# One of seven self-feature products by matmuls of 64 and 128 output columns in place of 32

## Chip, cores and metric

The kernel runs on one core of a Trainium2 chip. The metric is the device time of one execution in microseconds, the median of several runs. All data are 32-bit floats, apart from an integer adjacency.

## What is computed

The reference is a graph-attention layer over 16 batches, each with N = 512 nodes and F = 512 features. Cut to what matters:

```
q_exp     = where(x.sum(-1) == 0, 0, q)                  # (B, N, Q)
self_feat = concat([x, q_exp], -1) @ W_self.T + b_self   # (B, N, F)
output    = self_feat
for d in range(2):                                       # the two directions of the adjacency
    kv  = self_feat[:, :20]
    aff = (self_feat @ Wq[d].T + bq[d]) . (kv @ Wk[d].T + bk[d]) per head / sqrt(32)
    aff = where(mask_d, aff, -9e15) + label_bias_d       # 16 heads, 20 keys
    w   = softmax(aff, -1)
    output += (w @ kv) @ Wout[d] per head + bout[d]
out = x + relu(output)
```

The change touches the largest dense product in it, the part of self_feat that multiplies x with the first 512 columns of W_self.

## The kernel before

A setup of about 90 us loads the weights and works out for all 16 batches what depends only on the 20 key nodes: the keys folded into the query weights, the values folded into the output weights, and the self features of batch 0. The setup uses matmuls of several widths: 128 output columns (`key_rows`, line 581; `row_flags`, line 186; part of `values`, line 644), 64 (the other part of `values`, line 644) and 32 (`self_feat`, line 202). "Output columns" are the columns of the stationary operand, so they are the partitions of PSUM that the matmul writes.

Then a loop runs over batch `b` and over four tiles `nt` of 128 nodes each. The order of the instructions on every engine is the order of the program text (`manual_schedule`). For a pair (b, nt) TensorE does, in this order:

- nt = 0: `product(b, 4)`, `scores` (line 353), `product(b, 3)`
- nt = 1: `scores`
- nt = 2: `attend(b - 1)` (line 426, the weighted values of the batch before), `scores`, `product(b + 1, 1)`, `product(b + 1, 2)`
- nt = 3: `product(b + 1, 6)`, `scores`, `product(b + 1, 7)`, `product(b + 1, 5)`

`scores` issues 64 matmuls of 32 output columns and 152 moving columns. VectorE, ScalarE and GpSimd turn a tile of scores into weights by a softmax, and `turn` transposes them for `attend`. `attend` issues 24 matmuls on 32 of the 128 rows, 16 of them 32 columns wide and 8 of them 64 wide.

Self features of batch b + 1 are made in the loop during batch b, by seven products in the manner of Strassen and Winograd: W and the 492 nodes beyond the first 20 are cut in two by two blocks, of 256 x 256 weights and 256 x 246 inputs, and seven block products take the place of eight. `product` (line 279) makes one block product: `i` counts the two 128-row halves of the output, `k` the two halves of the contraction, and `a` four strips of 32 output columns, which write the four groups of 32 PSUM partitions. So a product is 16 matmuls, in the order (i, k) = (0,0), (0,1), (1,0), (1,1) with four strips each. Product 2 has a PSUM bank of its own, `ps_d`; `joined` (line 296) on VectorE reads it in nt = 3. The other products add up in `ps_a` and `ps_c`.

[...] The strips of one (i, k) appear pass by pass: four records of the first pass almost at once, then four of the second. In what follows a *pass* is such a group of strips that run beside each other. A batch has 392 matmuls, or 1568 records, and about 10 semaphore instructions on TensorE, 1578 in all.

The product loop before, whose strips are `R` = 32 columns wide (`HL` = 4 of them, `P` = 128):

```
for i in range(2):
    for k in range(2):
        for a in range(HL):
            at = i * P + a * R
...
            nc.tensor.matmul(to, lhs, x[:, k], start=start, stop=stop, skip_group_check=n != 2)
```

Of the kernel before, what the change touches and what calls it, by code (L numbers as in the profile page):

```python
# [13 lines left out]
P = 128  # L14
# [4 lines left out]
def gat_kernel(  # L19
# [21 lines left out]
    B, F, N = xT.shape  # L41
# [3 lines left out]
    HL = P // DH  # L45
# [6 lines left out]
    R = P // HL  # L52
    HN = (N - NG) // 2
# [12 lines left out]
    def bank(name, at=None):  # L66

        tag = {} if at is None else {"bufs": 1}
        return acc["pool"].tile([P, 512], F32, tag="acc" if at is None else f"acc{at}", name=name, **tag)
# [3 lines left out]
    ws_v = const.tile([P, C, F], F32, name="ws_v")  # L73
    ws_s = const.tile([P, 4, 2, F // 2], F32, name="ws_s")
# [17 lines left out]
    sums, parts, us, done = {}, {}, {}, {}  # L92
# [139 lines left out]
    def x_block(b, j, l):  # L232
        return xs[b][:, 2 * j : 2 * j + 2, half(l)]
# [12 lines left out]
    def product(b, n):  # L246

        w, x = {
            1: ((0, 0), lambda: x_block(b, 0, 0)),
            2: ((0, 1), lambda: x_block(b, 1, 0)),  # L250
            3: (3, lambda: x_block(b, 1, 1)),
            4: ((1, 1), lambda: sums[b, 4]),
            5: (0, lambda: sums[b, 1]),
            6: (1, lambda: sums[b, 2]),
            7: (2, lambda: sums[b, 3]),
        }[n]
        x = x()
        if n == 1:
            parts[b, "a"] = [bank(f"ps_a{b}_{i}", i) for i in range(2)]
        if n == 2:  # L260
            parts[b, "d"] = bank(f"ps_d{b}", 2)
        if n == 5:
            parts[b, "c"] = bank(f"ps_c{b}", 3)
        for i in range(2):
            for k in range(2):
                for a in range(HL):
                    at = i * P + a * R
                    if isinstance(w, tuple):
                        lhs = ws_v[:, 2 * w[1] + k, bass.ds(w[0] * F // 2 + at, R)]
                    else:  # L270
                        lhs = ws_s[:, w, k, bass.ds(at, R)]
                    if n in (2, 3, 5):
                        to = parts[b, "d" if n == 2 else "c"][bass.ts(a, R), bass.ts(i, HN)]
                        start = k == 0 if n == 2 else (n, i, k) == (5, 0, 0)
                        stop = k == 1 if n == 2 else (n, i, k) == (3, 1, 1)
                    else:
                        to = parts[b, "a"][i][bass.ts(a, R), :HN]
                        start, stop = (n, k) == (1, 0), (n, k) == (4, 1)
                    nc.tensor.matmul(to, lhs, x[:, k], start=start, stop=stop, skip_group_check=n != 2)  # L279
# [489 lines left out]
    with tc.manual_schedule():  # L769
# [11 lines left out]
        for b in range(B):  # L781
# [7 lines left out]
            for nt in range(NT):  # L789
# [22 lines left out]
                if nt == 0:  # L812
                    if b == 0:
                        for g in range(2):
                            scores(b, nt, g, ps[g])
                        mask_sum(b, 1)
                    else:
                        mask_mul(b, 1)
                        product(b, 4)
                        for g in range(2):  # L820
                            scores(b, nt, g, ps[g], range(2))
                        normal(*prev)
                        partial(b, 4, 1, 0, block(b, 1, 0))
                        if more:
                            load_x(b + 1, range(2), done["exp"])
                            load_x(b + 1, range(2, C), done["partial"])
                        for g in range(2):
                            scores(b, nt, g, ps[g], range(2, C))
                        if more:
                            row_mask(b + 1)  # L830
                        mask_count(b, 1)
                        joined(b, 3, "c", 1, 1)
                        product(b, 3)
                        mask_sum(b, 1)
                        if more:
                            load_adj(b + 1, 0, done["masks"])
# [46 lines left out]
                if nt == 2:  # L883
                    if more:
                        mask_mul(b + 1, 0)
                    else:
                        full_add(b, NT - 1)
                    if b > 0:
                        banks = [bank(f"ps_o{b - 1}_{q}", q) for q in range(4)]
                        attend(b - 1, banks)  # L890
                        o = work.tile([P, C, N], F32, tag="o", name=f"o{b - 1}")
                        finish(b - 1, o, banks)
                        if b + 2 < B:
                            load_xn(b + 2, 0, done["add"])
                            load_xn(b + 2, 1, done["relu"])
                    normal(*prev)
                    for g in range(2):
                        scores(b, nt, g, ps[g])
                    if more:
                        product(b + 1, 1)  # L900
                        product(b + 1, 2)
                    s = weigh(b, nt, pair, (lambda: partial(b + 1, 1, 0, 0)) if more else None)
                    expo(s)
                    turn(*prev)
                    if b > 0 and more:
                        load_keys(b + 1, range(2), done["exp"])
                    if more:
                        full_add(b, NT - 1)
                    if b > 0:
                        for c in (0, 1):  # L910
                            residual(b - 1, c, o)
# [53 lines left out]
        b = B - 1  # L965
# [22 lines left out]
        for q in (2, 3):  # L988
            w = (NT - 1) * P
# [56 lines left out]
```

## Time and profile before

| | |
|---|---|
| median of 3 runs | 591.74 us (591.52 to 592.68) |
| the profiled execution, whole | 593.27 us |
| its span, first to last instruction | 591.5 us |
| TensorE matmuls busy | 578.7 us, 98% of the span |
| TensorE weight loads busy | 439.7 us, 74% |
| VectorE busy | 492.3 us, 83% |
| ScalarE busy | 395.6 us, 67% |
| GpSimd busy | 384.2 us, 65% |
| mean granted TensorE clock | 0.995 |

The page of the profile gives busy time by engine, the chain of work that ended last, and the costliest groups of instructions. A row of the timeline reads: start and duration in us, engine, line, operation, output<-inputs, rows*columns of the stationary operand, shape of the moving operand, and the number of records merged into the row. A matmul row lasts from its first record's start to its last record's modelled end; since matmuls overlap, the time that a stretch takes on TensorE is the distance from its start to the start of the next stretch. "issue" as a releaser stands for a wait that the profile can't put down to any semaphore.

### The profile page before, as it was taken

The page shows a single profiled execution, that of the slowest core. Times are in us where ns is not written, and L with a number is a line of the kernel's source. Part 1 is how long each engine was busy: PE and PEld are TensorE (multiplying, and loading weights), DVE is VectorE, ACT ScalarE, POOL GpSimd, SP SyncE. Part 2 cuts the span into 40 slices and gives each one's busy share as a digit, 9 for nine tenths or more (in the row PEclk, how much of TensorE's full clock was granted, in tenths as well). Part 3 has the DMA queues.
Part 4 walks back from the last instruction along what each step waited for, and adds up shares of the span by engine and source line. Part 5 has one row for each costly group of instructions (what it writes and reads, how often), then busy time and mean ns, then how long its engine had stood idle before and what let it go on. Part 6 is the DMA issues. An engine that isn't in the chain of part 4 may idle for free.

```text
span 591.5 us, 30038 instructions
## 1 busy us (share of the span) xinstructions
PE 578.7 (98%) x13180; PEld 439.7 (74%) x13180; DVE 492.3 (83%) x785; ACT 395.6 (67%) x1162; POOL 384.2 (65%) x351
## 2 busy tenths in 40 slices
PE   8999999999999999999999999999999999999994
PEld 6654547888978687787878787788787878787882
DVE  0495565889898888999999999888989898989896
ACT  1234644587877677768686868677787877777661
POOL 2315663638677675758686777675858677776774
PEclk9999999999999999999999999999999999999997
DMA  8998999857848485767676766757585748582503
GB/s 294 385 406 299 332 376 329 257 126 199 223 154 229 155 236 148 206 168 209 184 208 163 223 173 202 171 181 208 164 217 170 216 149 232 158 238 85 167 13 142
DMA packets 98129, 124.10 MB, mean 210 GB/s; under 512 B 19952, under 2 KB 70160, under 8 KB 95952
## 3 DMA queue, kind: packets, MB, share of 16 engines
q1 hardware_dynamic: 96752, 120.31, 67.1%
q8 instruction: 103, 1.69, 1.2%
q0 software_dynamic: 672, 1.36, 1.0%
q10 hardware_dynamic: 576, 0.53, 0.3%
q14 instruction: 26, 0.21, 0.1%
HBM read 82.30 MB, written 40.24 MB: 207 GB/s over the span
## 4 chain that ended last, share of the span: by engine, by line
PE 94%; DVE 3%; DMA 1%; issue 1%; ACT 0%; POOL 0%; SPq 0%; DVEq 0%; POOLq 0%; ACTq 0%
PE ps_s L353 44%; PE ps_a L279 17%; PE ps_c L279 8%; PE ps_o L426 6%; PE ps_d L279 4%; PE ps_v L644 3%; PE ps_k L581 3%; PE ps_sf L202 2%; DMA ws_q<-in_wsT 1%; PE ps_kv L532 1%; DVE o L435 0%; PE ps_nz L186 0%; DVE wt L415 0%; DVE ps_s L371 0%; DVE sm L406 0%
## 5 line engine op out<-in xcount | busy, mean ns | idle before, releaser
L353 PEld LDWEIGHTS ps_s<-g,sf 128*32 128x32 f32 x8192 | 264.0, 110 | 19.8 <-issue 12.2
L353 PE MATMUL ps_s<-g,sf 128*32 128x152 f32 x8192 | 277.3, 293 | 0.5 <-ACT st L684 0.5
L334 ACT COPY both<-add 32x80 f32<-32x80 f32 x512 | 130.9, 256 | 54.8 <-DVE add L325 49.0
L408 POOL TENSOR_TENSOR s<-s,sm 128x640 f32<-128x640 f32 x63 | 80.3, 1275 | 98.0 <-DVE sm L407 98.0
L341 POOL TENSOR_TENSOR full<-cq,both 128x640 f32<-128x640 f32 x64 | 100.1, 1565 | 30.3 <-issue 24.3
L314 ACT ACTIVATE prod<-adj,wb_sb 128x80 f32<-128x80 int32 x330 | 112.5, 432 | 0.0
L380 ACT ACTIVATE s<-s 128x640 f32<-128x640 f32 x63 | 46.5, 738 | 69.4 <-DVE s L375 69.0
L444 POOL TENSOR_TENSOR o<-o,x 128x512 f32<-128x512 f32 x60 | 75.9, 1285 | 0.0
L367 DVE TENSOR_TENSOR full<-ps_s,full 128x608 f32<-128x608 f32 x63 | 49.1, 779 | 32.1 <-PE ps_s L353 26.6
L406 DVE TENSOR_REDUCE sm<-s 128x32 f32<-128x640 f32 x63 | 50.9, 808 | 8.8 <-ACT s L380 8.6
L279 PE MATMUL ps_a<-t,ws_s 128*32 128x246 f32 x960 | 55.5, 370 | 0.0
L371 DVE TENSOR_REDUCE ps_s<-full 128x32 f32<-128x640 f32 x63 | 52.2, 828 | 2.2
L415 DVE STREAM_TRANSPOSE wt<-s 128x640 f32<-128x640 f32 x63 | 52.8, 839 | 0.1
L375 DVE TENSOR_TENSOR s<-full,ps_s 128x640 f32<-128x640 f32 x63 | 51.6, 818 | 1.1
L426 PE MATMUL ps_o<-wt,vd 32*32 32x512 f32 (+5 forms) x816 | 40.8, 581 | 3.7 <-DVE wt L400 2.0
L279 PEld LDWEIGHTS ps_a<-t,ws_s 128*32 128x32 f32 x960 | 32.2, 110 | 15.5
L325 DVE TENSOR_REDUCE add<-prod 128x80 f32<-128x960 f32 x32 | 36.8, 1150 | 6.3 <-ACT prod L314 4.4
L244 POOL TENSOR_TENSOR t<-x 128x492 f32<-128x492 f32 x30 | 34.4, 1148 | 10.1 <-DVE full L367 5.2
L439 ACT ACTIVATE o<-o,bo 128x512 f32<-128x512 f32 x60 | 38.2, 708 | 0.6 <-POOL biased L881 0.6
L435 DVE TENSOR_TENSOR o<-ps_o,sf 128x512 f32<-128x512 f32 x60 | 36.8, 672 | 1.0 <-PE ps_o L426 1.0
L286 DVE SCALAR_TENSOR_TENSOR u<-nz,qw,ps_a 128x246 f32<-128x246 f32 x90 | 36.6, 449 | 0.0
L244 POOL TENSOR_TENSOR t<-x,t 128x492 f32<-128x492 f32 x30 | 34.4, 1147 | 1.2
(238 smaller groups left out, 722.7 us busy)
## 6 DMA issues: line engine op xcount, KB each, us to landing
g_d<-st SPq DMA_DIRECT2D x16, 1064.0 KB, 5.9
g<-g_d SPq DMA_DIRECT2D x28, 608.0 KB, 5.2
out_T<-o SPq DMA_DIRECT2D x60, 256.0 KB, 4.7
xn<-in_xn SPq DMA_DIRECT2D x28, 512.0 KB, 3.6
x<-in_xT SPq DMA_DIRECT2D x28, 512.0 KB, 4.3
adj<-in_adj SPq DMA_DIRECT2D x32, 440.0 KB, 5.0
nz<-nz_d SPq DMA_DIRECT2D x14, 256.0 KB, 4.0
wk<-in_wkT SPq DMA_DIRECT2D x2, 1024.0 KB, 8.0
```

The lines of the kernel that those rows point to most:

```text
L244: nc.gpsimd.tensor_sub(t, one, two)
L279: nc.tensor.matmul(to, lhs, x[:, k], start=start, stop=stop, skip_group_check=n != 2)
L314: nc.scalar.activation(p[:, :, l], a[:, :, l], AF.Identity, scale=wb_sb[:, l : l + 1])
L334: nc.scalar.copy(adds[b, h][bass.ts(a, R), :, g], add[r].rearrange("p (t m) -> p t m", t=2))
L341: nc.gpsimd.tensor_add(f, cqs[b].unsqueeze(1).to_broadcast(shape), adds[b, nt // 2][:, nt % 2].unsqueeze(2).to_broadcast(shape),)
L353: nc.tensor.matmul(bank[bass.ts(a, R), bass.ts(j, WD // HL)], sfs[b][:, k, bass.ds(nt * P + (2 * g + j) * R, R)], keys[:, k, a], start=(k ...
L371: nc.vector.tensor_reduce(mx, f, AX.X, ALU.max)
L375: nc.vector.tensor_sub(s, f, mx.unsqueeze(3).to_broadcast(full))
L408: done["normal"] = nc.gpsimd.tensor_mul(s, s, sm.unsqueeze(3).to_broadcast(full))
L415: nc.vector.transpose(wts[b][:, nt], s.rearrange("p a h m -> p (a h m)"))
L426: nc.tensor.matmul(banks[a][bass.ds(at // 2 * DH, n * DH)].rearrange("p (t n) -> p t n", n=32), vd[r, bass.ds(at * DH, n * DH)], wt[r, :, ...
L444: nc.gpsimd.tensor_add(o[:, c], o[:, c], xs[b][:, c])
```

## The change

In `product`, the strips of product 2 become wider: 64 columns where i == k, 128 where i != k. So product 2 has 6 matmuls in place of 16: two of 64 columns, then one of 128, one of 128, and two of 64. The weights that are read, the PSUM cells that are written and the order of i and k stay as they were. The six other products keep strips of 32. A batch has 382 matmuls, 1528 records, and 1538 TensorE instructions with the semaphore instructions. Fifteen product 2 are made in the loop, one for each batch but the first. Nothing changes in the instructions of the other engines or in the setup.

```
-                for a in range(HL):
-                    at = i * P + a * R
+                wide = (2 * R if i == k else P) if n == 2 else R
+                for a in range(P // wide):
+                    at = i * P + a * wide
                     if isinstance(w, tuple):
-                        lhs = ws_v[:, 2 * w[1] + k, bass.ds(w[0] * F // 2 + at, R)]
+                        lhs = ws_v[:, 2 * w[1] + k, bass.ds(w[0] * F // 2 + at, wide)]
                     else:
-                        lhs = ws_s[:, w, k, bass.ds(at, R)]
+                        lhs = ws_s[:, w, k, bass.ds(at, wide)]
                     if n in (2, 3, 5):
-                        to = parts[b, "d" if n == 2 else "c"][bass.ts(a, R), bass.ts(i, HN)]
+                        to = parts[b, "d" if n == 2 else "c"][bass.ts(a, wide), bass.ts(i, HN)]
```

## The prediction

> **What bounds the kernel now.** I read the page first: busy time, the chain that ended last, and the DMA queues.
>
> ```profile
> span 591.5 us, 30038 instructions
> PE 578.7 (98%) x13180; PEld 439.7 (74%) x13180; DVE 492.3 (83%) x785; ACT 395.6 (67%) x1162; POOL 384.2 (65%) x351
> ...
> q8 instruction: 103, 1.69, 1.2%
> ...
> PE 94%; DVE 3%; DMA 1%; issue 1%; ACT 0%; POOL 0%; SPq 0%; DVEq 0%; POOLq 0%; ACTq 0%
> ```
>
> TensorE carries 94% of the chain. A busy TensorE isn't a bound by itself, so the second view is what TensorE waited for inside the loop (from 108 to 560 us):
>
> ```profile
> PE ps_o L426 <- issue: 1.4, 3, 0.5
> PE ps_d L279 <- issue: 0.8, 1, 0.8
> ```
>
> It waits for no other engine and no transfer, only four times for "issue". So a microsecond added to or taken from TensorE's stream in the loop reaches the end, and no slack elsewhere hides it. All 15 changed products lie there. Third, the timeline of TensorE around product 2 in one batch (start, duration, and so on):
>
> ```profile
> 139.85 1.88 PE L279 MATMUL ps_a<-x,ws_v 128*32 128x246 f32 x32
> 141.51 1.88 PE L279 MATMUL ps_d<-x,ws_v 128*32 128x246 f32 x32
> 143.17 1.89 PE L279 MATMUL ps_a<-t,ws_s 128*32 128x246 f32 x32
> ```
>
> From start to start a product takes 1.66 us for 32 records, which is 8 passes of four strips, 0.2075 us a pass. Weight loads lie beneath them.
>
> **Part 1: the streaming doesn't change.** The setup has passes of all three widths. Two visits of one width with different numbers of passes give the price of a pass, and what a visit costs beyond its passes:
>
> ```profile
> 27.04 0.29 PE L669 MATMUL ps_g(0, 0, 0, 0, 2)0_268<-khD,wq_sb 32*128 32x152 f32 x2
> 27.28 2.42 PE L581 MATMUL ps_k<-kvT,wk 128*128 128x320 f32 x8
> ...
> 41.62 1.98 PE L644 MATMUL ps_v<-wo_sb,kvT 128*128 128x512 f32 x4
> 43.53 0.40 PE L669 MATMUL ps_g(0, 3, 1, 1, 2)0_409<-khD,wq_sb 32*128 32x152 f32 x2
> 51.47 1.08 PE L644 MATMUL ps_v<-wo_sb,kvT 128*64 128x512 f32 x4
> 52.48 0.52 PE L669 MATMUL ps_g(1, 2, 0, 0, 2)0_500<-khD,wq_sb 32*128 32x304 f32 x2
> 56.36 1.12 PE L186 MATMUL ps_nz<-rx,ones 128*128 128x512 f32 x2
> 57.41 0.61 PE L202 MATMUL ps_sf<-x,ws_v 128*32 128x236 f32 x8
> 57.95 0.78 PE L669 MATMUL ps_g(1, 3, 1, 0, 2)0_552<-khD,wq_sb 32*128 32x304 f32 x4
> 71.62 1.80 PE L202 MATMUL ps_sf<-x,ws_v 128*32 128x236 f32 x32
> 73.35 0.40 PE L669 MATMUL ps_g(2, 3, 0, 1, 2)0_727<-khD,wq_sb 32*128 32x152 f32 x2
> 82.84 1.13 PE L186 MATMUL ps_nz<-rx,ones 128*128 128x512 f32 x2
> 83.90 1.94 PE L644 MATMUL ps_v<-wo_sb,kvT 128*64 128x512 f32 x8
> 85.77 0.40 PE L669 MATMUL ps_g(3, 2, 0, 1, 2)0_841<-khD,wq_sb 32*128 32x152 f32 x2
> ```
>
> - 128 wide, 512 moving columns: 4 passes take 43.53 - 41.62 = 1.91, 2 passes 57.41 - 56.36 = 1.05. A pass is 0.43, and 0.20 is left over.
> - 64 wide, two strips beside each other: 4 passes take 85.77 - 83.90 = 1.87, 2 passes 52.48 - 51.47 = 1.01. A pass is 0.43 again, 0.15 is left over.
> - 32 wide, 236 columns: 8 passes take 1.73, 2 passes 0.54. A pass is 0.199, 0.14 is left over.
>
> 0.43 for 512 columns and 0.199 for 236 lie on one line (0.83 ns a column), which gives 0.2075 for the 246 of a product: a pass costs the same at each width. Product 2 has two passes for each of its four (i, k) before and after, 8 in all. So 480 matmul records become 180, and the streaming time stays 1.66 us. The records taken away cost nothing where they were; they ran beside others.
>
> **Part 2: four switches of width are added, 0.64 us a batch.** The left-over is paid once per visit. One part is a wait as a width is left: the last pass of 152 columns begins at 27.04, streams for 0.13 (by the line above) and the next width's first record comes at 27.28, so about 0.1 is wait. The rest, 0.04 to 0.1, must be a longer first pass. It isn't the change of rows that costs: 82.84 to 83.90 (left for 64 wide) and 56.36 to 57.41 (left for 32 wide) keep 128 rows on both sides and still cost 0.2 beyond two passes. Before, product 2 was part of one long visit to width 32. Now there are a visit to 64, one to 128, another to 64, and a second visit to 32 after it: 0.15 + 0.20 + 0.15 + 0.14 = 0.64 us. Product 2 so takes 2.30 us; times 15, **+9.6 us**. The steps 64 to 128 and 64 to 32 with 128 rows don't occur in the trace. Bounds: at the cheapest visit for all four, 4 x 0.14 x 15 = 8.4; at the dearest, 4 x 0.20 x 15 = 12. I take the sum of the rows of the widths themselves.
>
> If the wait alone were paid, four switches would cost 4 x 0.1 = 0.4 us a batch, 6 us in all (a rival, below).
>
> The Trainium skill, "TensorEngine Tiling (Array Packing)", Key Properties, says that a change of the tiling mode drains the array; it gives no time and speaks of no longer first pass. The wait in the rows agrees with it, and by it alone the sum would have the 6 us in place of 9.6.
>
> **Part 3: the instruction fetch, -7.0 us.** The "issue" waits aren't spread evenly. TensorE's 26,360 records and q8's 103 packets make 256 to a packet. Rows of the stalls, and of an attention stretch (L426) without one:
>
> ```profile
> 108.40 1.84 PE L279 MATMUL ps_a<-x,ws_v 128*32 128x246 f32 x32
> 110.06 0.60 PE L279 MATMUL ps_d<-x,ws_v 128*32 128x246 f32 x8
> 111.43 1.45 PE L279 MATMUL ps_d<-x,ws_v 128*32 128x246 f32 x24 [0.77 <-issue]
> ...
> 194.95 1.11 PE L426 MATMUL ps_o<-wt,vd 32*32 32x512 f32 x25
> 196.45 2.10 PE L426 MATMUL ps_o<-wt,vd 32*32 32x512 f32 x23 [0.39 <-issue]
> 198.48 0.72 PE L353 MATMUL ps_s<-g,sf 128*32 128x152 f32 x16
> ...
> 265.23 1.01 PE L279 MATMUL ps_a<-x,ws_v 128*32 128x246 f32 x16
> 289.38 2.24 PE L426 MATMUL ps_o<-wt,vd 32*32 32x512 f32 x48
> 291.55 0.72 PE L353 MATMUL ps_s<-g,sf 128*32 128x152 f32 x16
> ...
> 326.18 0.60 PE L279 MATMUL ps_a<-x,ws_v 128*32 128x246 f32 x8
> 542.09 1.22 PE L279 MATMUL ps_a<-x,ws_v 128*32 128x246 f32 x20
> ```
>
> Between the stalls at 111 and 196 us I counted instructions: busy time and records by engine in that window, then TensorE's semaphore instructions in it, by line:
>
> ```profile
> 111.00:196.20 85.20, 84.64 (x2161) 70.55 (x2160) 76.26 (x118) 64.33 (x199) 56.55 (x52) 1.00 0.68 181
> ```
> ```profile
> L279 PEldq EVENT_SEMAPHORE  x17: 51/51/51, 111.5 to 182.2; - x17
> L353 PEldq EVENT_SEMAPHORE  x5: 51/51/51, 122.2 to 186.2; - x5
> L426 PEldq EVENT_SEMAPHORE  x9: 51/51/51, 132.6 to 194.4; - x9
> ```
>
> 2161 + 2160 + 31 = 4352 = 17 x 256 exactly. The stalls stand on a grid of 256 instructions. The packets of q8 around them (two windows of the DMA view, 108.9 to 109.1 and 193.9 to 194.1 us) confirm it:
>
> ```profile
> q8 instruction: 1, 0.02, 32.3%
> ```
> ```profile
> q8 instruction: 1, 0.02, 30.7%
> ```
>
> A packet begins at about 109.0 and TensorE resumes at 111.43; one at 194.0, resumed at 196.45: 2.45 us each time. So TensorE takes instructions in blocks of 256, and where a block is fetched late it stands still.
>
> What this costs: the first record of product 1 marks a batch. Two quiet batches, 265.23 to 326.18, take 30.475 each; all 14 periods, 108.40 to 542.09, take 433.69. 433.69 - 14 x 30.475 = **7.0 us** of stalls. They hit particular places: 198.48 - 194.95 = 3.53 for an attention stretch with a block boundary in it, 291.55 - 289.38 = 2.17 without.
>
> Where the boundaries fall depends on the length of a batch. 1578 = 6 x 256 + 42, so before, each batch moves the grid by 42 records, and in some six batches it sweeps every place, the attention stretch (96 records) among them. 1538 = 6 x 256 + 2: after, the grid moves by 2 a batch and stays put. Its place is known, since nothing ahead of the first product 2 changes: a boundary lies there 64 + 17 records and a few semaphores, about 84, after product 1's start. In the order after (product 1 64 records, product 2 24, product 6 64, scores 256, products 7, 5 and 4 192, scores 256, product 3 64, scores 256, attention 96, scores 256) the six boundaries lie at 84, 340, 596, 852, 1108 and 1364 from product 1's start, drifting by 30 at most in 15 batches: in products 1 and 2, in the nt = 3 scores, in product 4, and in the three other score stretches. None reaches the attention stretch, 1176 to 1272, where the waits above have three of the four long stalls. The fourth, at 110 us, is met by the change itself: with six passes and their switches ahead of it, the same record comes about 1.7 us after product 2's start in place of 0.4, later than the block is there (111.43 - 110.06 = 1.37). So I take all 7.0 back. Bounds: nothing back, if other places stall as readily; below nothing, a stall of up to 3.53 - 2.17 = 1.36 us in each of 15 batches, +20 us, if the grid were stuck on a bad place.
>
> The Trainium skill, "Runtime: NRT & Kernel Launch", Instruction fetch mechanics, has the 256-instruction blocks, but says that crossing one is mostly hidden. By it there'd be nothing to take back, and the sum would be +9.6; the rows with their exact 17 x 256 speak against "mostly hidden" for this kernel.
>
> **Sum.** 593.27 (the profiled execution: its span of 591.5, and 1.77 around it) + 9.6 - 7.0 = 595.9. The median of the runs is 1.53 lower than the profiled one. If that offset holds for both kernels, the median comes to 594.3; if it was stalls that the profiling lengthened, they're gone after and the median comes to 595.9. I take the middle, **595.1**; by the bounds of part 2 and a stall or two left, its own range is 593.2 to 598.
>
> **Rivals.**
> - *The stalls stay*, as many as before, at new places. For it: a late fetch depends on the traffic of the moment, and the boundaries now meet the same traffic each batch. Against: in the trace nearly all stalls lie at L426. 591.74 + 9.6 = 601.3.
> - *A switch costs only its wait*, the longer first pass being hidden: 6 us against 7.0 saved: 590.7, no change that can be told. For it: passes hide their loads within a width. Against: both parts are in the left-over of every visit.
> - *Faster*: switches among widths at 128 rows are free in the loop, if weight loads run far enough ahead there, and the quiet grid alone counts: 591.74 - 7.0 = 584.7. It decides once the four switches cost less than 7.0 / 15 = 0.47 us together. Against: 82.84 to 83.90 has the rows equal and pays.
> - *The change doesn't act*: wide matmuls are cut into strips again, 591.7. Rows L186 and L644 show wide ones as they are.
>
> **Chances.** Forecast 0.72, stalls stay or come anew 0.14, wait alone 0.07, free switches 0.05, no action 0.02. 0.2%, about what a measurement here can tell, is 1.2 us: faster 0.05, same 0.09, slower 0.86. The range goes from 593.2 to 600.5, into the lower part of the first rival.
>
> **What would show it.** Product 2 from its first record to the next product's: 2.30 us, against 1.66. Period: 31.1 us in every batch. Attention always 2.17. Records 300 fewer on PE, q8 101 packets. Wrong, if the stretch takes under 2.1 or over 2.5 us, or if "issue" waits at L426 or elsewhere go on.

## The result, and the profile after

The changed kernel takes 595.34 us (median of 6 runs, 594.06 to 597.72), the kernel before 591.5 us beside it. The ratio is 1.0075, with a 95% interval of 1.0054 to 1.0095. A second comparison, among the experiments below, has 595.6 and 590.95, ratio 1.0064 [1.0041, 1.0087]. (The ratios are estimated from the single runs and need not be those of the two medians.) The change makes the kernel about 4 us slower. The forecast was 595.1.

The page of the changed kernel, in the lines that answer to those of before:

```profile
span 593.3 us, 29438 instructions
...
PE 583.8 (98%) x12880; PEld 434.4 (73%) x12880; DVE 491.5 (83%) x785; ACT 395.5 (67%) x1162; POOL 384.3 (65%) x351
...
q8 instruction: 101, 1.65, 1.2%
...
PE 96%; DVE 3%; ACT 0%; issue 0%; POOL 0%; DVEq 0%; POOLq 0%; ACTq 0%
```

TensorE has 300 matmul records fewer (the trace shows each matmul of the program as two weight loads and two matmul records, and 15 batches have 10 matmuls fewer), and is busy 5.1 us longer. The 1% of "issue" has left the chain. The view of waits for TensorE between 108 and 566 us, which named L426 and L279 before, lists nothing at all now; the table of busy time by stretch says the same in one row (length, then busy time of TensorE, its weight loads, VectorE, ScalarE and GpSimd, then granted clock, DMA share and GB/s):

```profile
108.00:566.00 458.00, 458.00 (x11220) 355.47 (x11216) 411.18 (x634) 345.05 (x1044) 319.81 (x279) 1.00 0.62 184
```

TensorE is busy in 458.00 of 458.00 us: by these records, whose ends are modelled, it doesn't stand still once in fourteen batches. The granted clock is 1.00 there. The timeline of TensorE shows what it does in that time: the first product 1, one batch later the next, an attention stretch, and the last product 1 (lines have moved by one: L280, L354, L427).

```profile
107.61 1.84 PE L280 MATMUL ps_a<-x,ws_v 128*32 128x246 f32 x32
109.38 2.23 PE L280 MATMUL ps_d<-x,ws_v 128*64 128x246 f32 x12
111.54 1.87 PE L280 MATMUL ps_a<-t,ws_s 128*32 128x246 f32 x32
...
200.94 1.84 PE L280 MATMUL ps_a<-x,ws_v 128*32 128x246 f32 x32
...
225.73 2.24 PE L427 MATMUL ps_o<-wt,vd 32*32 32x512 f32 x48
227.90 1.37 PE L354 MATMUL ps_s<-g,sf 128*32 128x152 f32 x36
...
232.06 1.22 PE L280 MATMUL ps_a<-x,ws_v 128*32 128x246 f32 x20
...
543.28 1.84 PE L280 MATMUL ps_a<-x,ws_v 128*32 128x246 f32 x32
```

- The period from 200.94 to 232.06 is 31.113 at full resolution, and 13 of the 14 periods are that; one is 31.21. The quiet period before was 30.476, so **a batch pays 0.637 us**. The prediction had 0.64.
- The attention stretch from 225.73 to 227.90 is 2.17, as it is in all 15 batches. Before, five of them took 2.6 to 3.75.
- All periods, 107.61 to 543.28, make 435.67 against 433.69 before: 14 x 0.637 = 8.92 more for the switches, 7.03 less in stalls, 0.1 for the one longer period. The stretch behind the last product 1, which holds the fifteenth product 2, is 593.3 - 543.28 = 50.0 against 49.4; the first product 1 comes 0.79 earlier, which nothing in the change explains. 1.98 + 0.6 - 0.8 is the 1.8 between the spans.

Single records of the period at 200.94 show what the 0.637 is made of. A pass follows the one before it after 0.2075 us. The first pass of 64 in product 2 follows after 0.32 and lasts 0.26, the first of 128 follows after 0.31 and lasts 0.31, the first of the second 64 after 0.30 and 0.26, and product 6's first pass of 32 after 0.31 and 0.23; all others in products 1, 2 and 6 keep to 0.2075 (to 0.004). So each change of width has a wait of 0.09 to 0.11, and a first pass that is longer by 0.05 (64), 0.10 (128) or 0.02 (32). Together they make the 0.637.

So two effects of several us each, of opposite signs, leave 4 us between them. The experiments take them apart.

### The profile page after: what moved, and what is told of

Same layout as the page of the kernel before. It is cut to its first block, busy times and chain, and to the rows that moved or that the text cites. A ratio compares the mean times of both kernels' runs of the same rounds, so it can differ in the third digit from the quotient of the medians.

```text
span 593.3 us, 29438 instructions
## 1 busy us (share of the span) xinstructions
PE 583.8 (98%) x12880; PEld 434.4 (73%) x12880; DVE 491.5 (83%) x785; ACT 395.5 (67%) x1162; POOL 384.3 (65%) x351
## 3 DMA queue, kind: packets, MB, share of 16 engines
q0 software_dynamic: 672, 1.36, 1.1%
## 4 chain that ended last, share of the span: by engine, by line
PE 96%; DVE 3%; ACT 0%; issue 0%; POOL 0%; DVEq 0%; POOLq 0%; ACTq 0%
PE ps_s L354 44%; PE ps_a L280 17%; PE ps_c L280 8%; PE ps_d L280 5%; PE ps_o L427 5%; PE ps_v L645 3%; PE ps_k L582 3%; PE ps_sf L202 2%; PE ps_kv L533 2%; PE ps_warm L492 1%; DVE o L436 0%; PE ps_nz L186 0%; DVE wt L416 0%; DVE ps_s L372 0%; DVE sm L407 0%
## 5 line engine op out<-in xcount | busy, mean ns | idle before, releaser
L354 PEld LDWEIGHTS ps_s<-g,sf 128*32 128x32 f32 x8192 | 263.0, 110 | 20.2 <-issue 12.2
L354 PE MATMUL ps_s<-g,sf 128*32 128x152 f32 x8192 | 276.3, 293 | 0.5 <-ACT st L685 0.5
L280 PE MATMUL ps_a<-t,ws_s 128*32 128x246 f32 x960 | 55.8, 372 | 0.0
L280 PEld LDWEIGHTS ps_a<-t,ws_s 128*32 128x32 f32 x960 | 29.6, 110 | 19.6 <-POOL full L342 5.5
L427 PE MATMUL ps_o<-wt,vd 32*32 32x512 f32 (+5 forms) x816 | 36.6, 580 | 2.3 <-DVE wt L401 2.0
```

Source lines behind the costliest of these rows:

```text
L354: nc.tensor.matmul(bank[bass.ts(a, R), bass.ts(j, WD // HL)], sfs[b][:, k, bass.ds(nt * P + (2 * g + j) * R, R)], keys[:, k, a], start=(k ...
L427: nc.tensor.matmul(banks[a][bass.ds(at // 2 * DH, n * DH)].rearrange("p (t n) -> p t n", n=32), vd[r, bass.ds(at * DH, n * DH)], wt[r, :, ...
```

## Experiments on the price of a switch

The theory: each visit to a width is paid once, and the number of passes within it doesn't matter. Rivals are that only the wait is paid, that the price goes by the number of wide matmuls, and that it goes by the switches from and to 32 alone. The instrument is the quiet period (most of the 14 agree to 0.002 us).

**One visit to 128 in place of three visits.**

```
-                wide = (2 * R if i == k else P) if n == 2 else R
+                wide = P if n == 2 else R
```

> Product 2 by four matmuls of 128 columns, so one visit to 128 in a long stretch of 32, and 1530 TensorE instructions a batch. Theory (a switch of width costs a wait and a longer first pass, whatever the number of wide passes): 0.20 + 0.14 = 0.34 us a batch, period 30.48 + 0.34 = 30.81 us. The block boundaries now drift by 6 records a batch the other way and touch the first records of the attention stretch only in the last two periods, so 12 of 14 periods are quiet, the last two within 0.7 of it. Against before: 15 x 0.34 - 7.0 + 0 to 1.4 = -2 to -0.6 us, about 589.5 to 591 by the median. Rival (wide passes are dearer in themselves): 8 wide passes where the changed kernel has 4, so over 0.64 us a batch, period 31.2 or more.

**One visit to 64.**

```
-                wide = (2 * R if i == k else P) if n == 2 else R
+                wide = 2 * R if n == 2 else R
```

> Product 2 by eight matmuls of 64 columns, 1546 TensorE instructions a batch. Theory: one visit to 64 and one more to 32, 0.15 + 0.14 = 0.29 us a batch, quiet period 30.77. Boundaries drift by 10 a batch, from record 84 down; they reach the attention stretch from its end in the period that begins with batch 8 (counted from 0) and stay in it to the end. So periods 0 to 7 quiet at 30.77 and periods 8 to 13 longer by 0.4 to 1.6 each. Rival (stalls vanished because TensorE has fewer records or more time, not because of where the boundaries lie): all 14 periods at 30.77.

**Three switches.**

```
-                wide = (2 * R if i == k else P) if n == 2 else R
+                wide = (P if i else 2 * R) if n == 2 else R
```

> Product 2 with its first input half by matmuls of 64 outputs and its second by matmuls of 128: 6 matmuls for 32, 1538 instructions in a batch as in the changed kernel, and three switches of width (32 to 64, 64 to 128, 128 to 32) in place of four. By switches: 0.15 + 0.20 + 0.14 = 0.49 us in a batch, a quiet period of 30.96 us, and 595.3 - 15 x 0.15 = 593.0 us. If the price were that of a switch to or from 32 alone (two of them in both kernels), the period would stay at 31.11 less nothing, 595.3 us.

**One visit to 64, longer, at 1538 instructions.** The last of the four (i, k) of product 1 is made by two matmuls of 64 (four records), so that the visit begins there; a batch again has ten matmuls fewer than before, and the block boundaries lie where the changed kernel has them.

```
-                wide = (2 * R if i == k else P) if n == 2 else R
+                wide = 2 * R if n == 2 or (n, i, k) == (1, 1, 1) else R
...
-                        to = parts[b, "a"][i][bass.ts(a, R), :HN]
+                        to = parts[b, "a"][i][bass.ts(a, wide), :HN]
```

> Product 2 wholly by matmuls of 64 outputs (8 in place of 32), and of product 1 before it the last of the four (head group, input half) pairs by 4 matmuls of 64 in place of 8 of 32... so that there is one visit to 64 and none to 128, and a batch has again 1538 TensorE instructions, with the block boundaries at the records where the changed kernel has them. If each visit to a width has its price, the quiet period between two batches is that of the kernel before plus one visit to 64: 30.476 + 0.289 = 30.77 us, 0.35 less than the changed kernel's 31.113, and no batch is longer than another, since no boundary lies in the attention; in all 595.3 - 15 x 0.346 = 590.2 us, about 0.2% under the kernel before (591.5). Rival, that a batch's price comes with the number of matmuls that are wide and not with the visits: 30.9 to 31.1. Rival, that the even periods of the changed kernel come from its slower product 2 and not from where the boundaries lie: single periods of 31.2 to 32 as in the all-64 kernel, 592 to 594 us.

A quiet period in each, as two rows of the timeline (first with product 1 and product 2, then the next product 1). The kernel with all of product 2 at 128:

```profile
200.42 1.84 PE L280 MATMUL ps_a<-x,ws_v 128*32 128x246 f32 x32
202.19 1.93 PE L280 MATMUL ps_d<-x,ws_v 128*128 128x246 f32 x8
...
231.23 1.84 PE L280 MATMUL ps_a<-x,ws_v 128*32 128x246 f32 x32
```

The kernel with product 2 at 64:

```profile
199.88 1.84 PE L280 MATMUL ps_a<-x,ws_v 128*32 128x246 f32 x32
201.66 1.88 PE L280 MATMUL ps_d<-x,ws_v 128*64 128x246 f32 x16
...
230.65 1.84 PE L280 MATMUL ps_a<-x,ws_v 128*32 128x246 f32 x32
```

The kernel with three switches:

```profile
201.01 1.84 PE L280 MATMUL ps_a<-x,ws_v 128*32 128x246 f32 x32
202.78 2.08 PE L280 MATMUL ps_d<-x,ws_v 128*64 128x246 f32 x12
...
231.97 1.22 PE L280 MATMUL ps_a<-x,ws_v 128*32 128x246 f32 x20
```

The kernel with the longer visit to 64:

```profile
200.62 1.99 PE L280 MATMUL ps_a<-x,ws_v 128*32 128x246 f32 x28
202.44 1.83 PE L280 MATMUL ps_d<-x,ws_v 128*64 128x246 f32 x16
...
231.38 1.43 PE L280 MATMUL ps_a<-x,ws_v 128*32 128x246 f32 x24
```

| product 2 | visits after width 32 | quiet period | over 30.476 | by the visits of the set-up | median, us | ratio to before |
|---|---|---|---|---|---|---|
| as changed | 64, 128, 64, 32 | 31.113 | 0.637 | 0.64 | 595.34 | 1.0075 [1.0054, 1.0095] |
| 64 then 128 | 64, 128, 32 | 30.961 | 0.485 | 0.49 | 593.73 | 1.0048 [1.0025, 1.007] |
| all 128 | 128, 32 | 30.810 | 0.334 | 0.34 | 594.49 | 1.005 [1.0031, 1.0068] |
| all 64 | 64, 32 | 30.765 | 0.289 | 0.29 | 594.37 | 1.0051 [1.0033, 1.007] |
| all 64, and a quarter of product 1 | 64, 32 | 30.763 | 0.287 | 0.29 | 590.71 | 0.9989 [0.9967, 1.001] |

Four sequences of visits in five kernels, one set of prices (0.15 for a visit to 64, 0.20 to 128, 0.14 to 32), and none is off by more than 0.006 us. The last two rows have the same visits with 16 and with 20 wide records: the price goes by the visit, not by the matmul. The step from two switches to three to four adds 0.15 to 0.2 each time, so it isn't the switches from and to 32 alone. The rows that the set-up didn't have, 64 to 128 and 64 to 32 at 128 rows, cost what the others do.

The totals of the two kernels with a single visit at other instruction counts missed: by price alone they'd be at about 590 to 591, and they took 594.4. Their quiet periods are right, but not all of their periods are quiet. In the all-128 kernel, four late ones are 31.97, 31.42, 31.74 and 30.99, where the expectation had two; in the all-64 kernel the later ones reach 32.0, and the first two are long as well, which the expectation had quiet. The first of these in each, as rows of the timeline; the all-128 kernel:

```profile
439.81 0.81 PE L354 MATMUL ps_s<-g,sf 128*32 128x152 f32 x14
441.22 0.46 PE L354 MATMUL ps_s<-g,sf 128*32 128x152 f32 x6 [0.60 <-issue]
441.61 2.24 PE L427 MATMUL ps_o<-wt,vd 32*32 32x512 f32 x48
```

The all-64 kernel:

```profile
108.40 1.05 PE L280 MATMUL ps_d<-x,ws_v 128*64 128x246 f32 x8
109.82 1.05 PE L280 MATMUL ps_d<-x,ws_v 128*64 128x246 f32 x8 [0.37 <-issue]
```

1530 = 6 x 256 - 6 and 1546 = 6 x 256 + 10, so in both the grid drifts, and comes to the attention in the late batches. In the all-64 kernel that isn't where most is lost: one attention stretch is longer (2.81), while the two longest periods, 32.00 and 31.59, lose 1.0 and 0.6 in product 7. The all-128 row shows the stall six records before the attention begins: the place need not be L427 itself. The all-64 row is the stall of before at 111 us, in the middle of the first product 2. The kernel with the longer visit to 64, back at 1538, loses 0.9 us to such stalls in all, and so comes out close to the 590.2 of its switches. It beats the changed kernel by 4.9 us, and can't be told from the kernel before.

## Experiments on the grid of 256

The theory: whether a batch stalls depends on where the block boundaries lie in it. Unused small matmuls in the set-up move the grid without touching the loop; 128 records put a boundary of the changed kernel into every attention stretch, 256 put the grid back where it was.

```
             warm = bank("ps_warm")
...
+            for _ in range(32):
+                nc.tensor.matmul(warm[:R, :8], ones[:, :R], ones[:, :8], start=True, stop=True)
```

The changed kernel with these 32 (128 records):

> The changed kernel with 32 unused matmuls (32 columns, 8 moving columns, 128 records) after the warm-up at the very start: nothing changes in the loop but where the 256-instruction boundaries lie. They move by 128 records and stand in the attention stretch, 52 to 22 records behind its start, in every batch. Theory: every period longer than 31.11 by 1.0 to 1.6 us, so 15 to 22 us over the changed kernel besides 1 to 5 us for the unused matmuls. Rival (TensorE's longer product 2 or its fewer records removed the stalls): all periods 31.11, only the unused matmuls added.

The kernel before with the same 32:

> The kernel before with the same 32 unused matmuls at the start. Theory: the stalls move by 128 / 42 = 3 batches. Of the 14 periods (0 to 13), those that were long were 0, 1, 2, 3, 8 and 9; now 0, 5, 6, 11 and 12 should be long (0.6 to 1.6 us over 30.48), 4 and 10 by up to 0.5, the rest quiet. Rival (stalls belong to certain batches, by their data or by the traffic there): the same periods as before are long.

The changed kernel with 64 of them (256 records), as the control:

> The changed kernel with 64 unused matmuls, 256 records, at the start: one whole block, so the boundaries stand where they stood in the changed kernel. Theory (the place of the boundaries decides): all 14 periods 31.11, and over the changed kernel only what the unused matmuls take at the start, twice the 3.5 us of 32 of them, about 602.5 us. Rival (the unused matmuls themselves upset the loop, by a shift in time against the loads): periods as uneven as with 128 records, 8 us more.

The changed kernel with 128 records more takes 608.11 us, ratio to before 1.0288 [1.025, 1.0326]: 12.8 us for 128 matmul records of 8 columns in the set-up. All 14 periods are longer than 31.113, from 31.23 to 33.28, together by 8.6 us, and the first product 1 is 3.55 later, 2.2 of it a stall just ahead of the loop. The control with twice as many has one period of 31.285 and 13 of 31.113; its 601.16 us, ratio 1.0174 [1.0146, 1.0202], is a set-up that is 4.6 longer (first product 1 at 112.19), with the loop as it was without them. The 4.6 are all there by 14.74 us, where the q weights' matmuls start (10.17 without the unused ones), and the granted clock is 0.5 for 3.41 us of that time. So it is not the matmuls, it is where they push the grid. The kernel before with 128 records more has its long periods (31.29 to 31.88) at the numbers 5, 6, 11 and 12, where unpadded they are 2, 3, 8 and 9 beside the first two (30.95 to 32.11). 128 is three batches of 42 records and 2 more, and they have moved by three (period 0, expected to be long too, is 0.34 over the quiet one); its one run of 598.55 us is used for its trace alone.

The size was expected at 15 to 22 us, and is 8.6: a stalled attention stretch was taken at the price of the kernel before's long ones (3.5 us), and a typical one here is this (timeline, then the view of the DMA queues for 325.5 to 325.7 us, then SyncE's issues):

```profile
326.78 0.82 PE L354 MATMUL ps_s<-g,sf 128*32 128x152 f32 x16
327.52 2.63 PE L427 MATMUL ps_o<-wt,vd 32*32 32x512 f32 x48
330.08 1.11 PE L354 MATMUL ps_s<-g,sf 128*32 128x152 f32 x28
```
```profile
q8 instruction: 1, 0.02, 30.6%
```
```profile
321.46 0.37 SPq L114 DMA_DIRECT2D adj<-in_adj  x1
325.21 0.34 SPq L175 DMA_DIRECT2D nz<-nz_d  x1
```

From 327.52 to 330.08 the attention takes 2.56, 0.39 over its 2.17. The instruction packet starts at 325.59; 2.4 later, at 327.98, TensorE goes on. The load of 440 KB that SyncE issued at 321.46 lands at 326.1, half a microsecond after the packet's start. That the packet stands behind that load is a guess so far; the next experiments try it.

Where the 8.6 us lie, from single records (a boundary counts as late, or on time by less than 0.1 us, where its first record starts no more than 0.1 us behind its packet's start + 2.45): 2.6 in the attention, where that holds for all 13 boundaries in batches 1 to 13, though four of the 14 stretches lose nothing; 4.4 with product 7, whose boundaries at records 440 to 464 of a batch are late in 8 of 13 (2.7 us in its own stretch, the rest mostly by the end of the scores of nt = 1). The prediction had looked at attention alone. Product 7 is the larger part here, and no boundary of the changed kernel lies in it.

The last 1.6 us lie in the first product 1, and no block is late there. Just behind the stall of 2.17 us ahead of the loop the granted clock, the third number from the end of this row, is 0.50 for 3.41 us:

```profile
110.94:114.35 3.41, 3.41 (x44) 2.12 (x35) 2.01 (x3) 0.83 (x3) 1.39 (x1) 0.50 1.01 309
```

The first product 1 takes 114.54 - 111.16 = 3.38 there in place of 1.77. The next three kernels below have 3.41 us at 0.5 too, at the end of such a stall or just behind it; the kernel before with 128 records more (a stall of 2.44) and the all-128 kernel with 64 records more (2.25) don't.

## Experiments on what makes a block late

A list of the loads under way as the packet starts has, in every late attention stretch, the first half of the next batch's adjacency (`adj`, 440 KB), issued 0.4 to 1.3 us ahead of the time when the block's turn to be fetched comes (above the table below is how that is told), and in every late product 7 the keys `g` (608 KB); but `g` is under way in the five product 7 that are on time as well. The theory: the packet waits behind that load. Rivals: it's the loads next to it (`cq`, and the adjacency's second half), or the place itself, whatever is loaded. The next three kernels have the 128 records more.

**The first adjacency load moved** to the end of nt = 3 of the batch before:

```
-                        if more:
-                            load_adj(b + 1, 0, done["masks"])
...
+                    if b + 2 < B:
+                        load_adj(b + 2, 0, done["exp"])
```

> The kernel with boundaries in every attention stretch (128 unused records), with the first load of the adjacency for batch b + 1 issued at the end of nt = 3 of the batch before, not in nt = 0. Theory A (the block fetch waits behind that 440 KB load, which is issued 18.6 us into a period, just ahead of the fetch): fetches for the attention boundary start 1 to 2 us after they are due, periods come down from a mean of 31.73 to within 0.15 of 31.11, total about 600. Theory B (the smaller loads issued in nt = 1 hold it up) or C (attention takes its instructions so fast that any boundary in it stalls): periods stay at a mean of 31.6 to 31.8, total about 608.

It takes 610.08 us, ratio to before 1.0304 [1.0278, 1.0329]; the total that the theory gave is missed. The attention is better (2.17 in ten of 15 batches, 2.2 to 2.5 in the others), but a boundary that was on time is late now: the one at records 952 to 976, in the scores of nt = 1, is late or within 0.1 us in 11 of 13 batches, where it was in 2. The moved load is now issued 1.0 to 1.7 us before that block's turn. The longest of these stalls in the timeline:

```profile
296.76 3.52 PE L354 MATMUL ps_s<-g,sf 128*32 128x152 f32 x101 [1.33 <-issue]
```

The stall has followed the load. That is what the theory says of the mechanism, and the opposite of what it was thought to be worth. One thing it doesn't fit: the moved load has landed 0.2 to 2.9 us before the late packets start. What is still under way then are the two loads of `x` (512 KB each) issued behind it; without the moved load ahead of them, the same loads left 11 of 13 of these packets on time. So a packet can be late behind a backlog of loads, and not by the one load alone.

**`cq` and the second half moved** behind the attention in nt = 2:

```
-                        load_cq(b + 1)
...
-                    if b > 0 and more:
-                        load_adj(b + 1, 1, done["normal"])
...
+                        if more:
+                            load_cq(b + 1)
+                            load_adj(b + 1, 1, done["add"])
```

> The same kernel with boundaries in every attention stretch; here the loads of cq and of the second half of the adjacency move from nt = 1 to behind the attention stretch in nt = 2, and the first adjacency load stays. Theory A: no change, mean period 31.6 to 31.8, total about 608. Theory B: periods near 31.11, total about 600. Theory C: no change.

610.32 us, ratio 1.0328 [1.0305, 1.0351], with the attention at 2.2 to 2.7 in 11 of 15 batches. This rival falls.

**The first adjacency load left out** from batch 2 on; batch 1's tile is used again, so that this part of the input isn't read:

```
-        t = adjs[b, h] = load.tile([P, 2, S * L], I32, tag="adj", name=f"adj{b}_{h}", bufs=3)
+        if h == 0 and b > 1:
+            adjs[b, h] = adjs[1, 0]
+            return
+        kept = (b, h) == (1, 0)
+        t = adjs[b, h] = load.tile(
+            [P, 2, S * L], I32, tag="adjk" if kept else "adj", name=f"adj{b}_{h}", bufs=1 if kept else 2
+        )
```

> The changed kernel with 128 more matmul records in the set-up (every block boundary falls into an attention stretch: 608.1 us), and without the load of the first half of the adjacency from batch 2 on (the tile of batch 1 is used again, so that this load of 440 KB is left out, and the result is not the reference's). Theory A, that the instruction block waits behind this load: the attention stretches lose their stalls, the periods come down to 31.11 (within 0.15) and the whole to 599 to 602 us, as in the kernel with 256 more records. Theory C, that the block waits behind whichever large load was asked for just before it, the next in line being those of x and of the second half: single periods of 31.4 to 32 stay, 602 to 606 us. Theory D, that the place in the attention alone makes the stall, whatever is loaded: 607 to 609 us as before.

607.37 us, ratio 1.027 [1.024, 1.0299]. By its total this is the rival of the place itself; by its trace it is not. The attention stretch of the batch shown above, with the packet's window (327.3 to 327.5 us):

```profile
331.45 2.24 PE L433 MATMUL ps_o<-wt,vd 32*32 32x512 f32 x48
333.62 1.63 PE L360 MATMUL ps_s<-g,sf 128*32 128x152 f32 x44
```
```profile
q8 instruction: 1, 0.02, 39.8%
```

The packet starts at 327.39, 4.1 us ahead of the attention in place of 1.9, and the stretch is 2.17. It is 2.17 in all 15 batches, with a boundary at the same records as before. The load is gone from the first period on (the first one left out is batch 2's, which was issued during batch 1). The 14 periods exceed 31.113 by 4.7 us together, against 8.6 with the load, each with the 1.6 of the clock in its first period; seven of the 14 are 31.11 to 31.12. Single periods of 31.4 to 32.1 stay, as the theory of whichever large load comes next had it, so that the first theory holds for the attention and not for all of the loop. What is left beside the clock goes with product 7, with the load of `g` under way, here in a timeline row and in SyncE's issues:

```profile
252.37 1.42 PE L286 MATMUL ps_a<-t,ws_s 128*32 128x246 f32 x22
254.14 0.81 PE L286 MATMUL ps_a<-t,ws_s 128*32 128x246 f32 x9 [0.35 <-issue]
```
```profile
247.08 0.38 SPq L136 DMA_DIRECT2D g<-g_d  x1
247.55 1.47 SPq L456 DMA_DIRECT2D out_T<-o  x2
251.38 0.38 SPq L136 DMA_DIRECT2D g<-g_d  x1
```

The total doesn't show the 3.9 us because the set-up has become longer: the last scores before the loop, in the padded kernel and then in this one,

```profile
110.29 1.18 PE L354 MATMUL ps_s<-g,sf 128*32 128x152 f32 x24 [2.17 <-issue]
111.16 3.45 PE L280 MATMUL ps_a<-x,ws_v 128*32 128x246 f32 x32
```
```profile
114.52 1.19 PE L360 MATMUL ps_s<-g,sf 128*32 128x152 f32 x24 [2.89 <-issue]
115.41 1.94 PE L286 MATMUL ps_a<-x,ws_v 128*32 128x246 f32 x16
```

come 4.2 us later, 0.7 of it in their own stall and 3.5 in the first 15 us of the set-up, as the unused matmuls and the first sixteen of line 535 (541 in this kernel) show, again in the padded kernel and then in this one:

```profile
4.33 2.50 PE L494 MATMUL ps_warm<-ones 128*32 128x8 f32 x64
6.76 4.58 PE L535 MATMUL ps_kv<-xkv,ws_v 128*128 128x320 f32 x16
```
```profile
4.33 3.58 PE L500 MATMUL ps_warm<-ones 128*32 128x8 f32 x64
7.84 6.99 PE L541 MATMUL ps_kv<-xkv,ws_v 128*128 128x320 f32 x16
```

The same matmuls take 3.5 us longer. The record of a granted clock of 1.0 begins at 5.12 in the first and at 12.75 in the second; before it there is no record. In the kernel before with 128 records more it begins at 13.77, and these sixteen take 7.49. So the set-up's part goes with how soon the full clock is granted. That the edit has to do with that isn't shown.

A table of the boundaries in batches 1 to 13, worked out from single records. A block's turn to be fetched is taken as the start of the record 320 ahead of its boundary: a mark of convenience, since no packet of the loop began sooner than 1.0 us after it. The columns are the range of records in a batch, the time that there is from the block's turn until TensorE is due at its boundary, and how many were late, or on time by less than 0.1 us:

| records | time there is | late, changed kernel | late, 128 more | late, 128 more and no first adjacency load |
|---|---|---|---|---|
| 56-80, 312-336, 568-592, 824-848, 1080-1104, 1336-1360 | 5.6-8.3 | 1 of 78 | - | - |
| 184-208, 696-720 | 6.9-8.3 | - | 2 of 26 | 0 of 26 |
| 440-464 (product 7) | 5.6-6.0 | - | 8 of 13 | 7 of 13 |
| 952-976, 1464-1488 | 5.7-6.4 | - | 2 of 26 | 0 of 26 |
| 1208-1232 (attention) | 5.0-6.1 | - | 13 of 13 | 0 of 13 |

Nearly all late blocks have both: 5 to 6 us in place of 7 to 8 to fetch them in, and a load of 440 or 608 KB issued about when their turn comes. The two late ones of the second row had over 7 us, and five of 13 in product 7 are on time in spite of `g`, so this is a tendency and not a rule. With the load gone, the attention's packets start 1.0 to 2.3 us after their turn in place of 2.6 to 3.7.

**The all-128 kernel with its grid moved off the attention.** 64 unused records, put where TensorE waits in the set-up:

```
+            for a in range(16):
+                nc.tensor.matmul(ps_q[bass.ts(a % HL, R), 1, 400:408], ones[:, :R], ones[:, :8], start=True, stop=True)
```

> Product 2 by four matmuls of 128 columns, and 16 unused matmuls (64 records, 8 moving columns) where TensorE waits for the q weights in the setup. The boundaries start 64 records earlier and drift by 6 a batch within 24 to 102, clear of the 146 to 166 where the kernel without them stalled in its last four periods. Theory: all 14 periods 30.81, 3.1 us less than without the unused matmuls, whose own time is hidden to within 1 us: 590.5 to 592.5 us, 3 to 5 under the changed kernel, and about even with the kernel before. Rival: stalls follow the last batches, 594.5.

594.35 us, ratio to before 1.0048 [1.0029, 1.0066], a miss. The late batches did become quiet (the last four periods are 30.81), but a boundary now lies in the first product 1, while the set-up's last loads are under way:

```profile
108.35 0.63 PE L280 MATMUL ps_a<-x,ws_v 128*32 128x246 f32 x8
111.22 1.45 PE L280 MATMUL ps_a<-x,ws_v 128*32 128x246 f32 x24 [2.25 <-issue]
```

One stall of 2.5 us took what the late batches gave back. The rival's 594.5 came out, but not for its reason.

**The changed kernel once more**, beside the kernel with three switches, the one with the longer visit to 64 and the one without the first adjacency load:

> The changed kernel once more beside the others: 595.3 us, periods of 31.113 us throughout.

595.6 us; 12 of its 14 periods are 31.112 to 31.114, the others, the first two, 31.156 and 31.218. The evenness of the changed kernel is not an accident of one execution.

## Why the prediction was right

- **TensorE bounds the kernel** (the first part): right. TensorE is busy without a break, and what a batch gains or loses there is in the period to the hundredth.
- **A pass costs the same at each width** (part 1): right. Product 2 at 64 and at 128 has the same eight passes, and the periods differ by 0.045 us, by the price of the visit alone.
- **Four switches at 0.64 us a batch, +9.6** (part 2): right in size, 0.637 and 9.56, and shown by four sequences of visits in five kernels. The two parts that it argued, a wait of about 0.1 and a first pass longer by 0.04 to 0.1, are there in single records: 0.09 to 0.11, and 0.02 to 0.10. (Its row of 128 gives 1.05 - 2 x 0.43 = 0.19 left over where it wrote 0.20; the sum changes by 0.01.) Where it lies was given wrongly. The stretch of product 2 was to take 2.30 us and takes 111.54 - 109.38 = 2.16; the stretch of product 1 ahead of it has gone from 1.66 to 109.38 - 107.61 = 1.77. The wait as a width is left comes before the first record of the next, so the first of these waits is in product 1's stretch; the rest, 0.02, is in product 6's first pass. The prediction put every wait into the stretch that follows it. Its test on the period was the sharper one.
- The Trainium skill's rule ("TensorEngine Tiling (Array Packing)", Key Properties: a change of the tiling mode drains the array) speaks of the wait alone, and the wait is there, 0.09 to 0.11 at each change of width; by the wait alone, 0.4, no period here comes out right. The rivals of the wait alone and of free switches fall with it.
- **-7.0 for the instruction fetch** (part 3): right in direction and nearly so in its cause, too large for the median. The profiled execution has got 7.03 - 0.1 back. But the medians differ by 595.34 - 591.5 = 3.8, and in the second comparison 4.65, so that in the median execution 9.56 - 3.8 = 5.7 or 9.56 - 4.65 = 4.9 came back. Before's profiled execution, at 593.27, is 1.8 us above its median. Of the two readings of that offset which the sum weighed, the first (an offset that both kernels have) doesn't hold: the changed kernel has a profiled execution of 595.05, not above its median, and that of its repeat is 595.56 against 595.6. The second (stalls which the profiled execution of before had beyond the median) fits, but with one trace of before it isn't shown. The middle that was taken made up for it; that the forecast came to within 0.3 us of the median is partly luck.
- **"None reaches the attention stretch"**: shown, by moving them there. That other places don't stall was an over-reading of before's trace: product 7 stalls as readily, and it was luck that 84 + 256 n misses both. "The stalls stay", the rival with 0.14, is what 128 records more would have made.
- **The stall at 111 us is met by the slower product 2**: borne out. It is gone in the changed kernel, and 0.37 us of idle time is back in the all-64 kernel, whose product 2 is faster. In the first execution of the changed kernel the packet also came sooner, 0.20 us behind product 1's first weight load in place of 0.69; in the repeat it came at 0.75, and that period is only 0.04 over 31.113.
- **The bound of 1.36 us for each stalled attention, +20**: too high; stuck on a bad place, the attention loses 0.56 us at most and 2.6 in 14 batches. Why before's long ones, with the same `adj` under way, lose 1.36 to 1.58 stays open.
- The Trainium skill, "Runtime: NRT & Kernel Launch", Instruction fetch mechanics, calls the crossing of a block mostly hidden. The prediction had its 17 x 256 speak against that; but most of the 16 boundaries between those two stalls cost nothing, so the kernel before agrees too. The changed kernel agrees (1 of 78 late or within 0.1 us); with 128 records more, 25 of 78 aren't, and the kernel is 12.8 us slower, 3.5 of it ahead of the loop and 1.6 by the halved clock in the loop's first product.

Open: what the packet waits for in the memory or the DMA engines, and why the loads of `x` (512 KB each), issued about when the turn of the block at records 952 to 976 comes, are harmless in 11 of 13 batches. That the attention's boundaries are late with the load of `adj` and not without it is shown by leaving it out; that also takes 440 KB out of the traffic at that time, and the two aren't told apart. For `g` it is argued from the loads under way, and was not tried.

## What to carry to other kernels

Fewer matmul instructions are no gain where TensorE streams without a break: count the passes, which stay, and the visits to a width, each of which has a price, so keep what is done at one width together. In a TensorE-bound loop, work out the number of TensorE instructions in an iteration modulo 256, and look where the boundaries fall and which large loads are issued just then; a change of ten instructions can be worth more by that than by its work. Compare whole periods, not the stretch that was edited, and look at the set-up and its granted clock too before a total is taken as a verdict on the loop.

## What was not expected of the hardware

- The price of a visit to a width hardly varies: 0.29 us for a visit to 64 and back to 32 (with 16 wide records and with 20), 0.33 to 128 and back, 0.15 more for a visit to 64 ahead of the one to 128 or behind it.
- An instruction block comes later with a load of 440 KB about: its packet starts 2.6 to 3.7 us after its turn, and 1.0 to 2.3 without the load. From the packet's start to TensorE's going on it is 2.2 to 2.5 us in the stalls of all these traces (the prediction's two had 2.45).
- With a stall of 2.2 to 2.9 us at the loop's start, four of six kernels show a granted clock of 0.5 for 3.41 us at its end or just behind it, and their first product 1 takes 0.9 to 1.6 us longer.
- 128 unused records of 8 columns in the set-up cost the changed kernel 12.8 us, 256 cost 5.8 (601.16 - 595.34; 4.7 between the profiled executions).
